# Transposes in row halves of the array over two PSUM banks, and the x1/x2 map once for two half-bands

## The chip, the cores and the metric

The kernel runs on one core of a Trainium2 chip. The metric is device time in microseconds (us), the median of the runs; lower is better. Engines are named as in the profile: PE (TensorE: PE its matmuls, PEld its weight loads), DVE (VectorE), ACT (ScalarE), POOL (GpSimd), SP (the queue that issues most transfers). Everything is float32.

## The reference, cut to what matters

Eight images of 256 channels, 64 x 64 pixels, go through two layers. `_gn` is a group norm without weights.

```python
def layer0(x):                        # on gn(x)
    x1, x2, x3 = w1 x + b1, w2 x + b2, w3 x + b3      # 1x1 maps to 32, 32 and 256 channels
    h = concat(x1, unfold3(reflect_pad(x2)))          # 32 + 288 channels
    h = relu(bn2(cw1 @ relu(bn1(h))))                 # 32 channels
    w = cw2 @ h + cb2                                 # 32 groups x 9 tap weights
    return sum over 9 taps of unfold3(zero_pad(x3)) * w     # 8 channels share a weight
def layer1(x):                        # on gn(x)
    q, k, v = 1x1 maps of x;  4 heads of 64
    att = softmax(q . (unfold7(reflect_pad(k)) + position)) # 49 neighbours of each pixel
    out_att = att . unfold7(reflect_pad(v))
    wts = softmax over 9 taps of (Wfc x)
    oc  = dwconv3(relu(dwconv3(x)))
    return rate1 * out_att + rate2 * sum(wts) * oc    # as the kernel factors it
x = x + layer0(gn(x));  x = x + layer1(gn(x))
```

## The kernel before

An image is cut into 8 bands of 8 rows (512 pixels), so there are 64 bands, counted by `g`. Each turn of the outer loop (L971) does layer 1 for band `g` and, beside it, layer 0 for band `g + 12` (`AHEAD`); the first 12 turns (`g < 0`) have layer 0 alone, the last 12 have no layer 0 left. A turn has 8 **slots**, `s = 4*ct + m`: `ct` is the half of the channels (two heads), `m` a pair of 8 x 8 pixel tiles. The order of all instructions on all engines is written out by hand (`tc.manual_schedule()`): `beside` and `steer` say what is put in the middle (`mid`) or at the end (`end`) of each slot, and `after(n, f)` puts `f` off by `n` calls of `advance()`. Each engine runs its own instructions in that order and never passes one that waits.

A slot of layer 1 puts this on PE, in order:

- `weighted_values` (L735): probabilities times values of an earlier tile pair, in 128 x 64 tiles of the array, two column halves in turn;
- `scores` (L691): queries times keys, in 64 x 64 tiles of the array;
- `transposed` (L723): the probabilities of the slot before, four transposes of 128 x 112 into one PSUM bank (`ptp`), evicted by one ACT copy to `pt` (L725);
- `branch_weights` (L813): four matmul instructions of 512 columns (one product of float32 is two instructions), `pf`, evicted by `exp` on ACT (L818);
- what stands in `mid`; `branch_weights` again; what stands in `end`.

`mid` and `end` hold, over the 8 slots of a band: queries `pq` and keys `pk` (for kb), values `pv` (evicted by several ACT copies to `vc`, L560 to L575), `value_tile` (four transposes of windows of the values, `pvt`, L595, evicted by one ACT copy to `vt`, L597), and of layer 0 the maps `p12` and `p3`, the hidden layer `ph` (L417) and the tap weights `pw` (L435). In an ordinary band `value_tile` stands in the middle of slots 0 and 1 and at the end of slots 6 and 7; `small_maps` (`p12`) stands in the middle of slot 0 behind `value_tile`, `value_maps` (`p3`) at the end of slot 0 and in the middle of slot 1, there behind `value_tile` too.

`small_maps` makes x2 three times and x1 once: `w12` has the columns [w2, w2, w2, w1], so one product of 128 output rows gives three copies of x2, which three ACT instructions write into the tile `x2` with the shifts left, none and right (L332), x1 by a fourth (L335), and two small ones write the reflected edge columns (L337, L338).

All PSUM tiles of PE's products but the scores share one pool, `tag="gen"`, of **five** buffers, each a bank of 2 KB per partition. A tile's first writer waits until the tile that had its bank before has been read.

The softmax of a slot goes PE scores -> DVE masked minimum (L700) -> ACT exp (L708) -> DVE reciprocal (L715) -> ACT scale (L717) -> PE transpose in the next slot. Once per `ct`, `dynamic_sum` (L820 to L849) runs over POOL and DVE, with two reciprocals of 256 columns.

Of the kernel before, what the change touches and what calls it, by code (L numbers as in the profile page):

```python
# [10 lines left out]
F32 = mybir.dt.float32  # L11
BF16 = mybir.dt.bfloat16
AF = mybir.ActivationFunctionType
# [5 lines left out]
P = 128  # L19
C = 256  # L20
NCT = C // P
H = W = 64
HW = H * W
R = 8
BAND = R * W
# [5 lines left out]
REL = 32  # L31
# [14 lines left out]
HD = C // HEADS  # L46
# [40 lines left out]
def conv_layers_kernel(ctx: ExitStack, tc: tile.TileContext, ins: dict, out: bass.AP):  # L87
# [19 lines left out]
    def load(name, shape, src=None, now=True):  # L107
        t = const.tile(shape, F32, name=f"c_{name}")
        late.append(lambda: nc.scalar.dma_start(out=t, in_=ins[name] if src is None else src))
        if now:  # L110
            late.pop()()
        return t
# [2 lines left out]
    par = load("par", [P, NPAR])  # L115
    chan = load("chan", [P, NCT, NCHAN], ins["chan"].rearrange("(t p) n -> p t n", p=P))
    rowp = load("rowp", [P, NROW], ins["rowp"].partition_broadcast(P))
    w12 = load("w12", [P, NCT, P], ins["w12"].rearrange("(t p) n -> p t n", p=P))
    w3 = load("w3", [P, NCT, C], ins["w3"].rearrange("(t p) n -> p t n", p=P))
    c1 = load("c1", [P, 3, REL])  # L120
    gq = load("gq", [P, P])
# [166 lines left out]
    def scaled_weights(b):  # L288

        im = images[b]  # L290

        def scale(sc, bi):
            im.w12s = w0.tile([P, NCT, P], F32, tag="w12s", name=f"w12s_{b}", bufs=1)
            im.w3s = w0.tile([P, NCT, C], F32, tag="w3s", name=f"w3s_{b}", bufs=1)
            for kt in range(NCT):
                nc.vector.tensor_scalar(im.w12s[:, kt], w12[:, kt], sc[:, kt : kt + 1], None, ALU.mult)
                nc.vector.tensor_scalar(im.w3s[:, kt], w3[:, kt], sc[:, kt : kt + 1], None, ALU.mult)
            after(5, lambda: through(bi))

        def through(bi):  # L300
            pb = ps.tile([P, 1 + NCT], F32, tag="gen", name=f"pb_{b}", bufs=5)
            for m, w in enumerate((w12, w3[:, :, :P], w3[:, :, P:])):
                for kt in range(NCT):
                    nc.tensor.matmul(
                        pb[:, m : m + 1], w[:, kt], bi[:, kt : kt + 1], start=(kt == 0), stop=(kt == NCT - 1)
                    )
            after(2, lambda: biases(pb))

        def biases(pb):
            im.bias = w0.tile([P, 1 + NCT], F32, tag="bias", name=f"bias_{b}")  # L310
            nc.vector.tensor_add(im.bias[:, 0:1], pb[:, 0:1], par[:, PB21 : PB21 + 1])
            for ct in range(NCT):
                nc.vector.tensor_add(
                    im.bias[:, 1 + ct : 2 + ct], pb[:, 1 + ct : 2 + ct], chan[:, ct, CB3 : CB3 + 1]
                )

        gn_affine([im.st0[:, ct] for ct in range(NCT)], gmat, f"a{b}", scale)

    def small_maps(b, i):


        im = images[b]
        p12 = ps.tile([P, BAND], F32, tag="gen", name=f"p12_{b}_{i}", bufs=5)
        for kt in range(NCT):
            nc.tensor.matmul(p12, im.w12s[:, kt, :], im.xc[i][:, kt, :], start=(kt == 0), stop=(kt == NCT - 1))  # L325
        p12 = p12.rearrange("p (r c) -> p r c", r=R)
        t = im.x2[i] = w0.tile([P, HR, W], F32, tag="x2", name=f"x2_{b}_{i}", bufs=2)
        bias = im.bias
        for q, (dst, src) in enumerate(((1, 0), (0, 0), (0, 1))):
            n = W - (q != 1)  # L330
            s = slice(32 * q, 32 * q + 32)
            nc.scalar.activation(  # L332
                t[s, 1 : 1 + R, dst : dst + n], p12[s, :, src : src + n], AF.Identity, bias=bias[s, 0:1]
            )
        nc.scalar.activation(t[96:128, 0:R, :], p12[96:128], AF.Identity, bias=bias[96:128, 0:1])  # L335

        nc.scalar.activation(t[0:32, 1 : 1 + R, 0:1], p12[0:32, :, 1:2], AF.Identity, bias=bias[0:32, 0:1])  # L337
        nc.scalar.activation(  # L338
            t[64:96, 1 : 1 + R, W - 1 : W], p12[64:96, :, W - 2 : W - 1], AF.Identity, bias=bias[64:96, 0:1]
        )  # L340

        if i == 0:
            nc.gpsimd.tensor_copy(t[0:96, 0, :], t[0:96, 2, :])
        else:
            nc.gpsimd.tensor_copy(t[0:96, 0, :], im.x2[i - 1][0:96, R, :])
            nc.gpsimd.tensor_copy(im.x2[i - 1][0:96, R + 1, :], t[0:96, 1, :])
        if i == NB - 1:
            nc.gpsimd.tensor_copy(t[0:96, R + 1, :], t[0:96, R - 1, :])
# [184 lines left out]
    def strided(v, at, *dims):  # L533

        return bass.AP(v.tensor, v.offset + at, [v.ap[0], *dims])

    def values(b, j, ct):
# [49 lines left out]
    def value_tile(b, j, u):  # L589
        im = images[b]  # L590
        n = min(R, WP - j * R) * KW
        pvt = ps.tile([CHUNK, 2, C], F32, tag="gen", name=f"pvt_{b}_{j}_{u}", bufs=5)
        for g in range(2):
            for ct in range(NCT):
                nc.tensor.transpose(pvt[:n, g, ct * P : (ct + 1) * P], im.vc[j, ct][:, 2 * u + g, :n], ident)  # L595
        vt = im.vt[j, u] = w1.tile([CHUNK, 2, C], F32, tag="vt", name=f"vt_{b}_{j}_{u}", bufs=9)
        nc.scalar.copy(vt[:n], pvt[:n])  # L597

    def new_keys(i):

# [71 lines left out]

        return finish

    half = [slice(0, HD), slice(HD, P)]
    turn = [0]

    def score_tile(nm):
# [38 lines left out]
            nc.scalar.activation(prob[:, h, :NKEY], prob[:, h, :NKEY], AF.Copy, scale=tot[:, h : h + 1])  # L717

    def transposed(nm, prob):
        ptp = ps.tile([CHUNK, 2, 2, P], F32, tag="gen", name=f"ptp_{nm}", bufs=5)  # L720
        for h in range(2):
            for ch in range(2):
                nc.tensor.transpose(ptp[:, h, ch], prob[:, h, ch * CHUNK : (ch + 1) * CHUNK], ident)  # L723
        pt = w1.tile([CHUNK, 2, 2, P], F32, tag="pt", name=f"pt_{nm}")
        nc.scalar.copy(pt, ptp)  # L725
        return pt

    def weighted_values(b, i, ct, m, pt, sco):
# [305 lines left out]
def _layout(inputs):  # L1034

    a = {k.replace("L0_conv_", "a_").replace("L1_conv_", "b_"): np.asarray(v) for k, v in inputs.items()}
    f = np.float32
    arr = {"x": a["x"].reshape(a["x"].shape[0], C, HW)}
    arr["w12"] = np.concatenate([a["a_w2"].T] * 3 + [a["a_w1"].T], axis=1)
    arr["w3"] = a["a_w3"].T  # L1040

    def branch(v):

        o = np.zeros((P, 3) + v.shape[1:], f)
        u = v[REL:].reshape((REL, 3, 3) + v.shape[1:])
        o[:96] = np.moveaxis(u, 2, 0).reshape((96, 3) + v.shape[1:])
        o[96:, 0] = v[:REL]
        return o

    arr["c1"] = branch(a["a_cw1"].T)  # L1050

    quarter = np.tile(np.eye(REL, dtype=f) / NQR, (NQR, 1))
    arr["gq"] = np.tile(quarter, (1, NQR))
    arr["gc"] = np.repeat(quarter, SHARE, axis=1).reshape(P, NCT, P)
    par = np.zeros((P, NPAR), f)
    for at, n in ((PG, "g"), (PB, "b"), (PM, "m"), (PV, "v")):
        par[:, at : at + 3] = branch(a[f"a_bn1_{n}"])
    par[:, PB21] = np.concatenate([a["a_b2"]] * 3 + [a["a_b1"]])
    for at, n in ((PG2, "g"), (PB2, "b"), (PM2, "m"), (PV2, "v")):
        par[:, at] = np.tile(a[f"a_bn2_{n}"], NQR)  # L1060
    par[:, PCB2 : PCB2 + KK] = np.tile(a["a_cb2"].reshape(REL, KK), (NQR, 1))
    arr["par"] = par

    c2 = a["a_cw2"].reshape(REL, KK, REL).transpose(2, 1, 0)
    arr["c2"] = np.zeros((P, KK, P), f)
    for q in range(NQR):
        arr["c2"][q * REL : (q + 1) * REL, :, q * REL : (q + 1) * REL] = c2

    chan = np.zeros((C, NCHAN), f)
    chan[:, CB3] = a["a_b3"]  # L1070
    chan[:, CBQ] = a["b_bq"]
    chan[:, CBK] = a["b_bk"]
    chan[:, CBV] = a["b_bv"]
    chan[:, CBP] = np.tile(a["b_bp"], HEADS)
    chan[:, CWP0 : CWP0 + 2] = np.tile(a["b_Wp"], (HEADS, 1))
    chan[:, CW1 : CW1 + KK] = a["b_w1"].reshape(C, KK)
    chan[:, CW2 : CW2 + KK] = a["b_w2"].reshape(C, KK)
    arr["chan"] = chan
    arr["wq"], arr["wk"], arr["wv"] = a["b_Wq"].T, a["b_Wk"].T, a["b_Wv"].T

    arr["wfc"] = a["b_Wfc"].reshape(C, KK, C)[:, [0, 1, 2, 3, 5, 6, 7, 8, 4]].transpose(2, 1, 0)

    loc = np.pad(np.linspace(-1.0, 1.0, W, dtype=f), PAD, mode="reflect")
    arr["rowp"] = np.concatenate(
        [loc, a["b_rate1"].reshape(1), a["b_rate2"].reshape(1)]
    )

    arr["gmat"] = np.kron(np.eye(P // 8, dtype=f), np.full((8, 8), 0.125, f))
    q, k = np.arange(NQ), np.arange(NKEY)
    dr = k[None] // KW - q[:, None] // TQ  # L1090
    dc = k[None] % KW - q[:, None] % TQ
    inside = (dr >= 0) & (dr < KA) & (dc >= 0) & (dc < KA)
    arr["mask"] = np.tile(np.where(inside, 0.0, NEG).astype(f), (2, 1))
    return {n: np.ascontiguousarray(v) for n, v in arr.items()}
# [19 lines left out]
```

## Time and profile before

| | us |
|---|---|
| median of 3 runs (4214.88 to 4219.61) | 4218.69 |
| span of the profiled run | 4215.3 |
| PE matmuls busy | 4079.7 (97%) |
| DVE busy | 3582.1 (85%) |
| ACT busy | 3046.5 (72%) |
| POOL busy | 2900.3 (69%) |
| granted TensorE clock, mean | 0.994 |

The busy time of PE counts from a matmul's start to its modelled end, so it holds pipeline latency and is not the rate of the work: the rate is read from the spacing of starts in the timeline. In the groups a row names the line, engine, operation, tile written and read, shape, count, then busy us and mean ns of one, then the idle time just before it and who ended it.

### The profile page before, as it was taken

The numbers are of one execution on the slowest core, as the hardware profiler recorded it, in microseconds if no ns is written. First come the engines' busy times: TensorE is split into PE (matmuls) and PEld (weight loads), VectorE is DVE, ScalarE is ACT, GpSimd is POOL, SyncE is SP. The second block draws the span as 40 slices with busy tenths as digits, with TensorE's granted clock in tenths as the row PEclk, the third lists the DMA queues.
The fourth block names the chain that finished last, engine by engine and source line by source line (L and its number), as shares of the span: only waits on it lengthen the run. The fifth ranks groups of instructions, "written<-read, shape, count | busy, mean of one in ns | idle before, by whom it ended". The sixth has DMA issues, their size and how long they took to land.

```text
span 4215.3 us, 72044 instructions
## 1 busy us (share of the span) xinstructions
PE 4079.7 (97%) x25004; PEld 2134.8 (51%) x25004; DVE 3582.1 (85%) x7244; ACT 3046.5 (72%) x7598; POOL 2900.3 (69%) x1778
## 2 busy tenths in 40 slices
PE   5889999999999999999999999999999999999998
PEld 2445555555555555555555555555555555555554
DVE  5778988888898898888988888888988888977777
ACT  3367778777777777877778777777778777677776
POOL 3657777677776777767777767767777777744445
PEclk9999999999999999999999999999999999999999
DMA  7753334233243333333333333343333233111100
GB/s 219 187 141 101 79 91 106 70 95 98 68 102 95 82 95 85 88 95 95 80 86 104 78 98 88 76 104 88 78 89 89 63 95 77 34 45 39 38 28 21
DMA packets 381260, 367.91 MB, mean 87 GB/s; under 512 B 55392, under 2 KB 282720, under 8 KB 380640
## 3 DMA queue, kind: packets, MB, share of 16 engines
q1 hardware_dynamic: 377568, 358.68, 33.4%
q8 instruction: 199, 3.26, 0.3%
q10 hardware_dynamic: 3328, 4.62, 0.3%
q14 instruction: 165, 1.35, 0.1%
HBM read 261.48 MB, written 101.71 MB: 86 GB/s over the span
## 4 chain that ended last, share of the span: by engine, by line
PE 74%; DVE 12%; POOL 7%; ACT 3%; issue 2%; SPq 2%; DMA 1%; POOLq 0%; ACTq 0%; DVEq 0%
PE pf L813 34%; PE ptp L723 6%; PE sco L735 5%; PE pk L646 5%; PE sco L691 5%; PE p L357 4%; POOL xg L456 4%; DVE prod L448 4%; PE pq L625 3%; PE pv L551 3%; PE pvt L595 2%; PE p L325 2%; PE pw L435 2%; POOL ex L1010 2%; DVE acc L796 2%
## 5 line engine op out<-in xcount | busy, mean ns | idle before, releaser
L813 PE MATMUL pf<-yp,c_wfc 128*128 128x512 f32 x4096 | 1932.4, 595 | 9.3 <-ACT vc L569 4.3
L456 POOL TENSOR_TENSOR xg<-xg,prod 128x1024 f32<-128x1024 f32 x549 | 1203.4, 2192 | 127.4 <-DVE prod L448 104.4
L813 PEld LDWEIGHTS pf<-yp,c_wfc 128*128 128x128 f32 x4096 | 733.8, 191 | 702.7 <-issue 658.9
L1010 POOL TENSOR_TENSOR ex<-ex,ex 128x1024 f32<-128x1024 f32 x384 | 907.7, 2364 | 61.9 <-ACT ex L818 57.2
L818 ACT ACTIVATE ex<-pf 128x512 f32<-128x512 f32 x1024 | 607.2, 593 | 335.7 <-PE pf L813 167.1
L770 DVE SCALAR_TENSOR_TENSOR acc<-yp,c_chan,acc 128x504 f32<-128x504 f32 (+3 forms) x1104 | 766.6, 694 | 47.7 <-ACT acc L761 27.1
L841 POOL TENSOR_TENSOR ex<-ex,rec 128x512 f32<-128x512 f32 x128 | 163.4, 1277 | 914.7 <-DVE rec L836 881.7
L796 DVE SCALAR_TENSOR_TENSOR acc<-hid,c_chan,acc 128x504 f32<-128x504 f32 (+3 forms) x1024 | 758.2, 740 | 20.2 <-ACT acc L790 2.1
L448 DVE SCALAR_TENSOR_TENSOR prod<-pw,c_par,x3q 128x1040 f32<-128x1040 f32 x576 | 734.4, 1281 | 46.3 <-PE pw L435 26.0
L717 ACT ACTIVATE prob<-prob,tot 128x196 f32<-128x196 f32 x1024 | 411.6, 450 | 467.9 <-DVE tot L715 467.9
L700 DVE CUSTOM_DVE_ANT_0 prob<-sco,c_mask 128x196 f32<-128x196 f32 x1024 | 325.1, 355 | 292.5 <-PE sco L691 292.0
L708 ACT ACTIVATE prob<-prob,nmax 128x196 f32<-128x196 f32 x1024 | 462.2, 456 | 46.9 <-DVE nmax L700 46.4
L735 PEld LDWEIGHTS sco<-pt,vt 112*64 112x64 f32 x8160 | 279.2, 137 | 209.5 <-issue 71.4
L723 PE MATMUL ptp<-ident,prob 128*112 128x128 f32 x2044 | 341.3, 287 | 26.4 <-ACT prob L717 25.9
L735 PE MATMUL sco<-pt,vt 112*64 112x64 f32 x8160 | 349.7, 228 | 0.0
L725 ACT COPY pt<-ptp 112x512 f32<-112x512 f32 x511 | 296.2, 580 | 70.5 <-PE ptp L723 66.5
L723 PEld LDWEIGHTS ptp<-ident,prob 128*112 128x112 f32 x2044 | 204.1, 133 | 194.0 <-ACT prob L717 69.4
L691 PE MATMUL sco<-kb,qb 64*64 64x196 f32 x4096 | 294.5, 357 | 0.2 <-DVE kb L661 0.2
L551 PE MATMUL pv<-yp,c_wv 128*128 128x512 f32 (+2 forms) x576 | 251.4, 561 | 0.0
L646 PE MATMUL pk<-yp,c_wk 128*128 128x512 f32 (+2 forms) x576 | 245.0, 552 | 0.0
L625 PE MATMUL pq<-yp,c_wq 128*128 128x512 f32 x512 | 242.2, 596 | 2.3 <-DVE prod L448 2.3
L357 PE MATMUL p<-xc,w3s 128*128 128x512 f32 x512 | 242.7, 598 | 0.0
(136 smaller groups left out, 5288.6 us busy)
## 6 DMA issues: line engine op xcount, KB each, us to landing
x<-x3n SPq DMA_DIRECT2D x128, 264.0 KB, 2.1
x3q<-x SPq DMA_DIRECT2D x128, 264.0 KB, 7.1
xc<-in_x SPq DMA_DIRECT2D x64, 512.0 KB, 5.0
xg<-in_x SPq DMA_DIRECT2D x256, 128.0 KB, 4.8
x<-xg SPq DMA_DIRECT2D x256, 128.0 KB, 2.4
yp<-x SPq DMA_DIRECT2D x128, 256.0 KB, 3.3
xr<-x SPq DMA_DIRECT2D x64, 512.0 KB, 5.7
out_x<-xr SPq DMA_DIRECT2D x64, 512.0 KB, 3.1
```

What stands on the lines that cost most here:

```text
L448: nc.vector.scalar_tensor_tensor(prod[:, :, :RUN], pw[:, j, :RUN].unsqueeze(1).to_broadcast([P, SHARE, RUN]), par[:, PCB2 + k : PCB2 + k + 1],
L456: nc.gpsimd.tensor_add(im.xg[i], im.xg[i], rows(prod))
L646: nc.tensor.matmul(pk[:, :n], wk[:, kt, ct * P : (ct + 1) * P], im.yp[i][:, kt, a : a + n], start=(kt == 0), stop=(kt == NCT - 1),)
L691: nc.tensor.matmul(sco[half[t], h, :NKEY], qb[half[h], 2 * m + t].rearrange("p r c -> p (r c)"), kb[half[h], :, c0 : c0 + KW], start=True, ...
L708: nc.scalar.activation(prob[:, h, :NKEY], prob[:, h, :NKEY], AF.Exp, bias=nmax[:, h : h + 1], scale=-1.0, accum_out=tot[:, h : h + 1],)
L723: nc.tensor.transpose(ptp[:, h, ch], prob[:, h, ch * CHUNK : (ch + 1) * CHUNK], ident)
L735: nc.tensor.matmul(po[half[h], :, t * TQ : (t + 1) * TQ], im.vt[i + ch, m][:n, t, (2 * ct + h) * HD : (2 * ct + h + 1) * HD], pt[:n, h, ch ...
L770: nc.vector.scalar_tensor_tensor(o, yp[:, ct, ra + dr : rb + dr, ca + dc : cb + dc], chan[:, ct, CW1 + k : CW1 + k + 1], o, ALU.mult, ALU.add,
L796: nc.vector.scalar_tensor_tensor(o, hid[:, ra + dr : rb + dr, ca + dc : cb + dc], chan[:, ct, CW2 + k : CW2 + k + 1], o, ALU.mult, ALU.add,)
L813: nc.tensor.matmul(pf, wfc[:, kt, 2 * m + j, ct * P : (ct + 1) * P], images[b].yp[i][:, kt, PAD : PAD + R], start=(kt == 0), stop=(kt == N ...
L818: nc.scalar.activation(ex[:, j].rearrange("p (r c) -> p r c", r=R), pf, AF.Exp)
L1010: after(4, lambda ex=ex, exb=exb: nc.gpsimd.tensor_add(ex, ex, exb))
```

## The change

Three edits, in the same places of the written order.

- `transposed` and `value_tile`: each transpose of 128 rows becomes two of 64 rows. The array is used in two row halves (64 x 128 tiles), upper and lower, one after the other in the instruction stream, so that the two can run side by side; each half writes its own PSUM bank, with 64 columns per transpose instead of 128. The one eviction of 512 columns becomes two of 256.
- `small_maps`: `w12` has the columns [w2, w1] once, 64 of them. The band is cut into two halves of 256 pixels, which go through two column halves of the array (128 x 64 tiles) into the lower and upper 64 partitions of one bank. ACT writes the three shifts and x1 from each half, eight instructions of half the columns; the two edge columns are now copied by POOL from the tile itself.
- The bias products (`pb`) follow the new layout, 8 times in the kernel.

It is for PE time: a transpose streams half the columns, and the map is not made three times over.

```diff
     def transposed(nm, prob):
-        ptp = ps.tile([CHUNK, 2, 2, P], F32, tag="gen", name=f"ptp_{nm}", bufs=5)
+        ptp = [ps.tile([CHUNK, 4, NQ], F32, tag="gen", name=f"ptp_{nm}_{t}", bufs=5) for t in range(2)]
         for h in range(2):
             for ch in range(2):
-                nc.tensor.transpose(ptp[:, h, ch], prob[:, h, ch * CHUNK : (ch + 1) * CHUNK], ident)
+                for t in range(2):
+                    nc.tensor.transpose(
+                        ptp[t][:, 2 * h + ch], prob[half[t], h, ch * CHUNK : (ch + 1) * CHUNK], ident[half[t], half[t]]
+                    )
         pt = w1.tile([CHUNK, 2, 2, P], F32, tag="pt", name=f"pt_{nm}")
-        nc.scalar.copy(pt, ptp)
+        for t in range(2):
+            nc.scalar.copy(pt.rearrange("p h c q -> p (h c) q")[:, :, t * NQ : (t + 1) * NQ], ptp[t])
         return pt
...
     def value_tile(b, j, u):
-        pvt = ps.tile([CHUNK, 2, C], F32, tag="gen", name=f"pvt_{b}_{j}_{u}", bufs=5)
+        pvt = [
+            ps.tile([CHUNK, 2 * NCT, HD], F32, tag="gen", name=f"pvt_{b}_{j}_{u}_{r}", bufs=5) for r in range(2)
+        ]
         for g in range(2):
             for ct in range(NCT):
-                nc.tensor.transpose(pvt[:n, g, ct * P : (ct + 1) * P], im.vc[j, ct][:, 2 * u + g, :n], ident)
-        nc.scalar.copy(vt[:n], pvt[:n])
+                for r in range(2):
+                    nc.tensor.transpose(
+                        pvt[r][:n, g * NCT + ct], im.vc[j, ct][half[r], 2 * u + g, :n], ident[half[r], half[r]]
+                    )
+        for r in range(2):
+            nc.scalar.copy(vt[:n].rearrange("p g (t r d) -> p (g t) r d", r=2, d=HD)[:, :, r], pvt[r][:n])
...
     def small_maps(b, i):
-        p12 = ps.tile([P, BAND], F32, tag="gen", name=f"p12_{b}_{i}", bufs=5)
+        p12 = ps.tile([P, R // 2, W], F32, tag="gen", name=f"p12_{b}_{i}", bufs=5)
         for kt in range(NCT):
-            nc.tensor.matmul(p12, im.w12s[:, kt, :], im.xc[i][:, kt, :], start=(kt == 0), stop=(kt == NCT - 1))
+            for u in range(2):
+                nc.tensor.matmul(
+                    p12[64 * u : 64 * u + 64], im.w12s[:, kt, :],
+                    im.xc[i][:, kt, u * BAND // 2 : (u + 1) * BAND // 2],
+                    start=(kt == 0), stop=(kt == NCT - 1),
+                )
-        for q, (dst, src) in enumerate(((1, 0), (0, 0), (0, 1))):
...
+        for u in range(2):
+            r, o = u * R // 2, 64 * u
+            for q, (dst, src) in enumerate(((1, 0), (0, 0), (0, 1))):
+                n = W - (q != 1)
+                nc.scalar.activation(
+                    t[32 * q : 32 * q + 32, r + 1 : r + 1 + R // 2, dst : dst + n],
+                    p12[o : o + 32, :, src : src + n], AF.Identity, bias=bias[o : o + 32, 0:1],
+                )
...
+        nc.gpsimd.tensor_copy(t[0:32, 1 : 1 + R, 0:1], t[0:32, 1 : 1 + R, 2:3])
+        nc.gpsimd.tensor_copy(t[64:96, 1 : 1 + R, W - 1 : W], t[64:96, 1 : 1 + R, W - 3 : W - 2])
```

## The prediction

> **What bounds the kernel now.** I read the engine shares and the chain first, then the groups that the edits touch, then the timeline of PE.
>
> ```profile
> PE 4079.7 (97%) x25004; PEld 2134.8 (51%) x25004; DVE 3582.1 (85%) x7244; ACT 3046.5 (72%) x7598; POOL 2900.3 (69%) x1778
> PE 74%; DVE 12%; POOL 7%; ACT 3%; issue 2%; SPq 2%; DMA 1%; POOLq 0%; ACTq 0%; DVEq 0%
> L723 PE MATMUL ptp<-ident,prob 128*112 128x128 f32 x2044 | 341.3, 287 | 26.4 <-ACT prob L717 25.9
> L725 ACT COPY pt<-ptp 112x512 f32<-112x512 f32 x511 | 296.2, 580 | 70.5 <-PE ptp L723 66.5
> ```
>
> PE sets the pace: on the chain for 74% of the span, and hardly waiting (26 us before all transposes). But DVE and POOL hold 19% of the chain, so PE meets them somewhere in each band. PE time therefore counts, and so does each new wait of PE. The timeline of PE (start, us, group) gives the prices:
>
> ```profile
> 2005.60 1.88 PE L813 MATMUL pf<-yp,c_wfc 128*128 128x512 f32 x4
> 2007.41 0.43 PE L417 MATMUL ph<-hid,c_c 96*32 96x128 f32 x8
> 2007.77 1.98 PE L551 MATMUL pv<-yp,c_wv 128*128 128x512 f32 x4
> 2009.59 1.88 PE L813 MATMUL pf<-yp,c_wfc 128*128 128x512 f32 x4
> 2011.40 0.69 PE L735 MATMUL sco<-pt,vt 112*64 112x64 f32 x16
> 2012.01 0.57 PE L691 MATMUL sco<-kb,qb 64*64 64x196 f32 x8
> 2012.52 0.65 PE L723 MATMUL ptp<-ident,prob 128*112 128x128 f32 x4
> 2013.00 1.88 PE L813 MATMUL pf<-yp,c_wfc 128*128 128x512 f32 x4
> 2014.72 1.88 PE L551 MATMUL pv<-yp,c_wv 128*128 128x512 f32 x4
> 2016.44 1.88 PE L813 MATMUL pf<-yp,c_wfc 128*128 128x512 f32 x4
> ```
>
> Starts, not durations, are to be read. Four 512-column instructions without a change of tile shape take 1.72 (2014.72 to 2016.44), 0.429 each. Where the next group has another shape they take 1.81 (2005.60 to 2007.41, 2009.59 to 2011.40): **a change of tile shape costs 0.09**. The group after one pays its first weight load too: `pv` after `ph` takes 1.82 instead of 1.72, 0.10 for a 128-column load. The four transposes take 0.48: 0.05 for the first load of 112 columns, then 4 x 0.109. Sixteen instructions of 64 columns in two column halves (L735) take 0.61: 0.05 load, 8 pairs at 0.058, 0.09 change. Two tile halves do run side by side.
>
> **What the Trainium skill says.** "TensorEngine Tiling (Array Packing)", Key Properties: changing the tiling mode drains the engine, changing only the tile doesn't. The trace agrees: 0.09 at each change, nothing between the halves of L735. "TensorE: Matmul & The Clock Gate", Part 3 (The mechanism): matmuls and loads in different row groups overlap; the scores agree (8 instructions in four tiles, two row halves among them, in 0.51, where one stream of 8 x 196 columns at L735's rate would need 1.4). The Tiling page, Gotcha 1, lets different row tiles write only different banks at one time: hence the second bank. "ScalarE: Activation LUTs", What ACT_TABLE_LOAD costs: a fixed part per instruction, about 280 ns with a pointer bias, before 0.833 ns an element; this trace has 265 ns for 8 elements (L338) and 580 for a copy of 512.
>
> **The change part by part.**
>
> *Transposes of probabilities, 511 groups.* Body 4 x 0.109 = 0.436 becomes 4 pairs x 0.058 + 0.006 = 0.24: -0.20. The entry comes from the scores' 64 x 64 tiles and pays 0.09 + 0.05 already. The exit is new: `pf`, today loaded behind the last transpose, now pays 0.09 + 0.10: +0.20. Sum 0.
>
> *Transposes of values, 288 groups.* Body -0.196 x 288 = -56. In the built order 271 of them follow 128 x 128 work and now pay 0.09 + 0.05 at the entry: +39. Of the exits 128 go into L735, which changes shape today as well; 97 go into 128 x 128 work, +0.197 each: +19; 45 go into `p12`, counted there. Sum +2.
>
> *The map of x1 and x2, 64 times.* Four times 0.429 = 1.72 becomes 8 instructions of 256 columns in pairs, 4 x 0.216 = 0.86; entry 0.09 + 0.05, exit 0.09 + 0.10. Net -0.51. The 12 in the turns without layer 1 aren't on PE's path (PE is busy 190 of the first 269 us): 52 x -0.51 = -26.
>
> PE's own work: about -24 us.
>
> *ACT.* A copy of 128 x 252 takes 353 ns in the trace, one of 512 columns 580. Two halves are about 0.72: +0.14 a group, 799 groups, +112 us. `p12`: today 2 x 672 + 680 + 679 + 2 x 265 = 3.23; eight of 256 columns at 265 + 0.82 x 250 = 470 are 3.76: +34 us in all. ACT goes from 3046 to about 3190, 76%. It is not the bound, but it is later wherever PE waits for it. The two POOL copies of an edge column take at most the 0.23 of the 96 x 64 copy in the trace, 30 us on an engine 69% busy: hidden beside the products.
>
> *Banks.* This is the part that sets the sign. The pool has five, and a transpose group now takes two, so a tile gets a bank that was handed out fewer tiles ago. I took each tile's bank in the built program of the changed kernel and, with the times of before, the end of the last read of its former tenant against the start of its first write. In an ordinary band all but a few keep 0.6 us or more; those that come out negative stand in the same slots of every band:
>
> ```profile
> 2338.13 0.81 ACT L717 ACTIVATE prob<-prob,tot 128x196 f32<-128x196 f32 x2 [5.18 <-DVE tot L715]
> 2338.64 0.78 PE L723 MATMUL ptp<-ident,prob 128*112 128x128 f32 x4 [1.16 <-ACT prob L717]
> 2339.26 1.88 PE L813 MATMUL pf<-yp,c_wfc 128*128 128x512 f32 x4
> 2339.92 0.34 ACT L569 COPY vc<-pv 128x16 f32<-128x16 f32 x3
> 2347.11 0.58 ACT L818 ACTIVATE ex<-pf 128x512 f32<-128x512 f32 x1
> 2347.26 1.98 PE L813 MATMUL pf<-yp,c_wfc 128*128 128x512 f32 x4
> 2347.59 0.58 ACT L597 COPY vt<-pvt 112x512 f32<-112x512 f32 x1
> ```
>
> ACT stands for 5.18 us behind DVE's reciprocal, then works off what has piled up. In slot 6 `pf` (2339.26) gets the bank of `pv`, read until 2340.26: PE starts it at 2340.4. In slot 7 the second transpose tile gets the bank of slot 6's second `pf` (read until 2347.69) and `pf` that of the first half of `pvt` (until about 2347.95). So transposes end near 2348.0, and `pf` streams at 2348.2 after drain and load, where today it streams at 2347.37: **+0.83 a band**, since ACT and DVE here wait for no PE and don't move. Queued behind these waits is all of PE; who waits for PE comes later and moves with it. With bands 0 to 5 of images 0 to 6: 42 x 0.83 = +35. In bands 6 and 7 the gaps are -0.45 and -0.5: +7.
>
> In band 0 ACT waits for DVE in front of the copies of two value tiles:
>
> ```profile
> 2284.47 0.65 PE L723 MATMUL ptp<-ident,prob 128*112 128x128 f32 x4
> 2286.33 0.22 ACT L776 ACTIVATE hid<-acc 128x64 f32<-128x64 f32 x1 [1.65 <-DVE acc L770]
> 2287.22 1.06 ACT L597 COPY vt<-pvt 112x512 f32<-112x512 f32 x2
> ```
>
> The second `ptp` gets the bank of a half of `pvt`, free at about 2287.6: PE stands from 2284.5 on, +3.1; 8 images, +25. Last, `pf` of slot 1 gets the bank of `p12`, whose ACT reading ends about 1 later (0.14 + 0.14 + 0.53 and a little queueing) while PE arrives 0.5 sooner; the gap of 1.24 becomes about -0.25: 52 x 0.25 = +13.
>
> Waits: +80. Sum: 4218.7 - 24 + 80, about **4273 us**.
>
> **The rivals.**
>
> *PE's saving stands, the waits don't come* (faster). For it: PE waits little today, and my gaps hold ACT's times fixed. Against: at the two places ACT is held by DVE, not by PE. 4218.7 - 24 = 4195.
>
> *ACT becomes the pace in the crowded slots.* For it: L725 waits only 66 us for PE today, so ACT is often behind; two fifths of the 146 us added to it might then reach PE, 60. Against: in the stage from 1000 to 3500 it is busy 1876 of 2500. 4273 + 60 = 4335.
>
> *The halves don't run side by side* (the two row halves take turns): 8 x 0.058 = 0.46 a body instead of 0.24, 799 x 0.225 = +180: 4450. Against: the scores use row halves side by side.
>
> *Gain and waits cancel*: a third of the waits (26) would do: about 4220.
>
> **How the numbers follow.** My forecast 0.60, ACT pacing 0.14, no side by side 0.07: slower 0.81. Waits absent 0.14: faster. Cancelling: same 0.05. Unknown costs: a pair at 0.055 to 0.07 moves the sum by -10 to +38 us, a half copy at 0.33 to 0.42 moves ACT by -48 to +96 us, of which waits pass on perhaps half. The range 4190 to 4335 takes in the first rival and the unknown costs and leaves out the 4450 and the upper part of ACT's case.
>
> **What would show it.** Right: starts of L723's successor 0.24 + 0.05 after its own group, plus 0.19 before the next stream; the count of such exits at 511; waits of PE before `ptp` and `pf` put down to ACT (`vt`, `vc`, `ex`) of some 80 us more than today, about 0.8 in slot 7 of each band and 3 in slot 0 of each image's first; `p12` in 0.86. Wrong: pairs at 0.11 (no overlap), no 0.09 at the exit (then faster by up to 100 us), or PE's waits unchanged.

## The result, and the profile after

| | before | after |
|---|---|---|
| median, us | 4219.15 | 4279.4 |
| lowest and highest run | 4214.88 to 4219.94 | 4277.57 to 4281.49 |
| span of the profiled run | 4215.3 | 4276.7 |
| granted TensorE clock, mean | 0.994 | 0.985 |

The ratio is 1.0145, with a 95% interval of 1.0127 to 1.0163: the changed kernel is slower by 60 us. The forecast was 4273. Each column has four runs; for the kernel before that is one run more than ahead of the prediction, so its median is 4219.15 instead of 4218.69.

The lines of the page of the changed kernel that answer to those shown of before (engine shares, chain, groups):

```profile
PE 4080.4 (95%) x28492; PEld 2042.7 (48%) x28492; DVE 3586.4 (84%) x7244; ACT 3127.8 (73%) x8526; POOL 2925.0 (68%) x1906
PE 52%; DVE 24%; POOL 10%; ACT 6%; issue 4%; DMA 2%; SPq 2%; POOLq 0%; DVEq 0%; ACTq 0%
L746 ACT COPY pt<-ptp 112x256 f32<-112x256 f32 x1022 | 326.3, 373 | 58.3 <-PE ptp L741 57.9
L741 PE MATMUL ptp<-ident,prob 64*112 64x64 f32 x4088 | 247.1, 231 | 53.8 <-ACT vt L614 19.3
```

PE's busy time hardly changed (4079.7 to 4080.4) although the map costs less. PE's share of the chain fell from 74% to 52%, so it now waits in places where it did not wait before. The transposes stand 53.8 us before they start (26.4 before). The list of PE's waits (what waits, for whom, us in total, times, longest) of the changed kernel says for whom:

```profile
PE pf L834 <- ACT vc L579: 35.8, 36, 1.0
...
PE ptp L741 <- ACT vt L614: 19.3, 7, 2.8
PE ptp L741 <- ACT prob L733: 14.3, 16, 2.3
PE ptp L741 <- ACT ex L839: 7.1, 33, 0.4
```

The same lines of the kernel before:

```profile
PE ptp L723 <- ACT prob L717: 25.9, 51, 2.7
...
PE pf L813 <- ACT vc L569: 4.3, 6, 0.7
```

Only `prob` is data that the transposes read. `vc`, `vt` and `ex` are ACT's copies *out of* the banks that PE wants to write: these are waits for a bank, 36 of them of 1.0 us behind the values' copies (6 of at most 0.7 us before), 7 of 2.8 us behind the value tiles. The prediction had named both banks. One of the 36, in the timeline of the changed kernel, first PE and then ACT:

```profile
2374.32 0.67 PE L741 MATMUL ptp<-ident,prob 64*112 64x64 f32 x8 [1.12 <-ACT prob L733]
2375.99 3.52 PE L834 MATMUL pf<-yp,c_wfc 128*128 128x512 f32 x4 [0.99 <-ACT vc L579]
2379.30 2.08 PE L642 MATMUL pq<-yp,c_wq 128*128 128x512 f32 x4
```

```profile
2366.27 0.68 ACT L746 COPY pt<-ptp 112x256 f32<-112x256 f32 x2
...
2373.81 0.81 ACT L733 ACTIVATE prob<-prob,tot 128x196 f32<-128x196 f32 x2 [5.14 <-DVE tot L731]
2374.53 0.70 ACT L570 COPY vc<-pv 128x672 f32<-128x672 f32 x1
2375.25 0.31 ACT L575 COPY vc<-pv 128x176 f32<-128x176 f32 x1
2375.60 0.34 ACT L579 COPY vc<-pv 128x16 f32<-128x16 f32 x3
```

The first ACT line, two half evictions, is used further down. The products of this `pv` had started at 2367.81 and PE went on to its next group at 2369.53, but ACT copied them only from 2374.53 on: the scale ahead of them waited 5.14 us for DVE's reciprocal. `pf` starts at 2375.99, when the last `vc` copy (2375.60 + 0.34) has emptied the bank of `pv`. There is a second thing to see, which no step of the prediction has: from the start of this `pf` to the next group pass 3.31 us, where the same four instructions took 1.82 elsewhere. PE runs at half its clock here. The table by stretches, with the granted clock in the column before the DMA share, shows it: first the changed kernel,

```profile
core 0: us, PE busy (x) PEld busy (x) DVE busy (x) ACT busy (x) POOL busy (x), PEclk, DMA share, GB/s
...
2318.00:2321.40 3.40, 3.18 (x10) 1.63 (x11) 3.25 (x7) 2.42 (x10) 2.40 (x2) 0.54 0.80 215
2376.00:2379.40 3.40, 3.40 (x5) 1.39 (x6) 3.40 (x8) 3.17 (x9) 2.30 (x2) 0.54 0.02 5
```

then the kernel before in the second stretch:

```profile
2376.00:2379.40 3.40, 3.40 (x34) 1.80 (x33) 3.30 (x9) 3.40 (x7) 3.32 (x3) 1.00 0.99 320
```

**Where the time went.** Two sums over the whole trace carry the rest of this document. *Waits*: for each of the 511 transpose groups, the time from the start of the scores before it to the start of `pf` behind it, less the median of all groups of that kernel. (This takes in a wait before the first transpose, between two of them, and before `pf`.) *Half clock*: the time at a granted clock of 0.5, without the first 300 and the last 20 us; each costs PE half of itself at most. All rows but `before` and `after` are kernels of the experiments below; an interval is mostly 3.4 us long, some are 6.8.

```
                         median   waits   of which in:             half clock
                         us       us      slots 6, 7  band 0,      us (intervals)
                                                      slots 0, 1
before                   4219      55.5      54.2        0.0         3.4  (1)
map_only                 4194.5    55.5      53.8        0.3         6.8  (1)
ptp_only                 4252.1    85.1      80.4        0.7        30.7  (8)
pvt_only                 4280.7    92.1      71.3       18.1        23.9  (6)
two_banks                4294.7   104.0      82.6       18.9        47.8 (13)
two_copies               4216.5    55.1      53.7        0.0         3.4  (1)
after                    4279.4   128.5      93.3       24.0        61.4 (17)
values_first             4307.5   130.3      97.5       22.2       109.2 (31)
late_scale               4230.3    85.6      51.6       23.8        47.8  (8)
tiles_first              4257.7   112.5      94.5        7.4        41.0  (9)
late_scale_tiles_first   4202.1    68.5      51.3        6.5         3.4  (1)
before_late_tiles        4204.0    46.2      43.6        0.0         0.0  (0)
map_late_tiles           4179.8    45.8      43.2        0.5         3.4  (1)
```

From before to after: waits +73, half clock (61.4 - 3.4) / 2 = +29 at most, PE's own work about -39 (52 maps at -0.507, 511 transpose groups at -0.0175, and in 52 bands the value tiles, with slot 1 longer by 0.125 and slots 0, 6 and 7 shorter by 0.07 each: -4). That makes +63 at most where the span grew by 61; some 2 us of the half-clock cost lie inside the groups whose waits are summed, and are counted twice.

### The profile page after: what moved, and what is told of

It reads as the page before. It is cut to its first block, busy times and chain, and to the rows that moved or that the text cites. A ratio compares the mean times of both kernels' runs of the same rounds, so it can differ in the third digit from the quotient of the medians.

```text
span 4276.7 us, 79947 instructions
## 1 busy us (share of the span) xinstructions
PE 4080.4 (95%) x28492; PEld 2042.7 (48%) x28492; DVE 3586.4 (84%) x7244; ACT 3127.8 (73%) x8526; POOL 2925.0 (68%) x1906
## 4 chain that ended last, share of the span: by engine, by line
PE 52%; DVE 24%; POOL 10%; ACT 6%; issue 4%; DMA 2%; SPq 2%; POOLq 0%; DVEq 0%; ACTq 0%
PE pf L834 26%; POOL xg L464 5%; DVE prod L456 5%; PE pk L663 5%; DVE acc L817 4%; DVE acc L791 4%; PE p L365 4%; PE sco L756 4%; PE pq L642 3%; PE sco L707 3%; POOL ex L1031 3%; DVE ex L852 3%; PE ptp L741 2%; DVE rec L853 2%; POOL ex L845 1%
## 5 line engine op out<-in xcount | busy, mean ns | idle before, releaser
L834 PE MATMUL pf<-yp,c_wfc 128*128 128x512 f32 x4096 | 2013.7, 615 | 42.8 <-ACT vc L579 35.8
L746 ACT COPY pt<-ptp 112x256 f32<-112x256 f32 x1022 | 326.3, 373 | 58.3 <-PE ptp L741 57.9
L741 PE MATMUL ptp<-ident,prob 64*112 64x64 f32 x4088 | 247.1, 231 | 53.8 <-ACT vt L614 19.3
L741 PEld LDWEIGHTS ptp<-ident,prob 64*112 64x112 f32 x4088 | 164.0, 131 | 221.0 <-issue 54.1
```

What stands on the lines that cost most here:

```text
L741: nc.tensor.transpose(ptp[t][:, 2 * h + ch], prob[half[t], h, ch * CHUNK : (ch + 1) * CHUNK], ident[half[t], half[t]])
L834: nc.tensor.matmul(pf, wfc[:, kt, 2 * m + j, ct * P : (ct + 1) * P], images[b].yp[i][:, kt, PAD : PAD + R], start=(kt == 0), stop=(kt == N ...
```

## The experiments

Theories for the loss: **B** (banks), PE waits for banks because a transpose group takes two of the five; **A** (ACT), the larger number of ACT instructions is the price; **R** (row halves), the changes of tile shape cost more than the shorter transposes save. Each ratio is to runs of the kernel before made beside that run (medians 4217.81 to 4219.2).

**The map alone** (`map_only`): before with the edits to `small_maps`, `w12` and `pb` and no others.

> The map of x1 and x2 alone in its new form, the transposes as before. My theory: PE saves 0.51 us in each of the 52 bands that have layer 1 beside it, no tile gets a bank sooner than before but for small shifts, so 4219 - 26, about 4193 (4188 to 4200). Rival, that the longer ACT reading of the map's bank takes the gain back in slot 1: 4210 or more.

4194.52 us (4192.56 to 4199.17), ratio 0.9946 (0.9933 to 0.9958). As expected: slot 0 of an ordinary band is 0.507 us shorter, and the waits stay at 55.5. This part of the change is a gain in full.

**The transposes of probabilities alone** (`ptp_only`): before with the edit of `transposed` and no others.

> The transposes of probabilities alone in row halves over two banks. My theory: PE -9 us (511 x 0.017, from the trace after), waits of about 0.45 us at slot 7 in 42 bands (+20) and about 1.1 us in the first band of each image (+9), so about 4240 (4228 to 4255). Rival, that the new changes of tile shape are what costs and not the banks: the waits of PE for ACT stay as before and the spacing behind each transpose group is over 0.3 us longer than the body saves.

4252.07 us (4251.37 to 4254.49), ratio 1.0081 (1.0067 to 1.0094). Within the expected range, but not by the expected sum. Slots without a wait are 0.017 us *shorter*, so a group's gain in the body and its exit nearly cancel, and the waits are +29.6 as expected, though nearly all in slots 6 and 7 (+26) and hardly any in band 0 (+0.7, where 9 were expected). The rest is seven more half-clock intervals, (30.7 - 3.4) / 2 = 14 us, which were not expected.

**The transposes of values alone** (`pvt_only`): before with the edit of `value_tile` and no others.

> The transposes of values alone in row halves over two banks. My theory: PE's own work -3 us, waits of 2.8 us in slot 0 of each image's first band (+23), 0.44 us at slot 7 in 42 bands (+18), so about 4257 (4240 to 4268). Rival, that all of the loss hangs on the probabilities, which are twice as many: 4220.

4280.65 us (4279.66 to 4281.57), ratio 1.0147 (1.0133 to 1.0161): 24 us over what was expected, and outside the range. A line of its list of waits:

```profile
PE ptp L731 <- ACT qb L638: 42.8, 41, 1.2
```

In slot 7 the transposes now wait for the bank that ACT's copy of the queries (`qb`) empties. The waits grew by 36.6, half of that in band 0, half in slots 6 and 7; 41 were expected. So the miss lies elsewhere. Alone, PE's own work is not level but about +10 by the prediction's own prices: 271 entries at 0.14 are +38, and of exits into full-shape work there are now 142 (97 and the 45 into the unchanged `p12`) at 0.197, +28, against -56. Slots 0 and 1 show it, each 0.125 us longer. With the half clock's 10 that is 57 of the 63; the other 6 stay open.

**Two banks without row halves** (`two_banks`): the kernel before, with four full-height transposes spread over two banks and two evictions, for the probabilities as shown and for `value_tile` likewise.

```diff
-        ptp = ps.tile([CHUNK, 2, 2, P], F32, tag="gen", name=f"ptp_{nm}", bufs=5)
+        ptp = [ps.tile([CHUNK, 2, P], F32, tag="gen", name=f"ptp_{nm}_{t}", bufs=5) for t in range(2)]
...
-        nc.scalar.copy(pt, ptp)
+        for h in range(2):
+            nc.scalar.copy(pt[:, h], ptp[h])
```

> Kernel before, with each group of four full-height transposes spread over two banks and evicted by two ACT copies: the banks and the copies of the change without its row halves and without any new change of tile shape. My theory (the banks set the sign): all waits of the changed kernel come, 42 x 0.9 + 8 x 3 + 7, so about 4289 (4270 to 4300). Rival (the row halves and their shape changes cost the time): 4219 to 4225.

4294.74 us (4292.9 to 4298.19), ratio 1.0182 (1.0166 to 1.0197). The two largest bank waits of the changed kernel are there, in the same counts, in its list of waits:

```profile
PE pf L815 <- ACT vc L569: 28.0, 36, 0.8
...
PE ptp L724 <- ACT vt L598: 15.9, 7, 2.3
```

PE's instructions are those of the kernel before (only the order of the four transposes differs), the tile shape changes nowhere else than it did before, and yet it loses 77 us. R is out as the cause of the loss. (That the new exits eat the gain of the shorter transposes is so: `ptp_only` has -0.017 a group left of 0.20.) The 4289 that was expected was met partly by luck: the waits grew by 48.5 and not by 69, and the half clock adds (47.8 - 3.4) / 2 = 22.

**Two evictions, one bank** (`two_copies`): before, with each eviction of a transpose group (`ptp` and `pvt`) cut in two, the bank as it was.

```diff
-        nc.scalar.copy(pt, ptp)
+        for h in range(2):
+            nc.scalar.copy(pt[:, h], ptp[:, h])
```

> Kernel before, with every eviction of a transpose group cut into two ACT copies from the same one bank: the added ACT work of the change without a second bank. My theory: ACT works 80 to 110 us more in all, and PE hardly sees it: 4216 to 4225. Rival (ACT's added work is what PE waits for): half of it comes through, 4260 or more.

4216.45 us (4213.48 to 4219.15), ratio 0.9996 (0.9987 to 1.0005): nothing. The copies of the groups take 48 us more on ACT than before, as they do in the changed kernel (47); its whole busy time rose by 43, less than the expected 80 to 110. `map_only` holds the rest of ACT's added work, without a loss. A is out. The second bank is what `two_banks` has and `two_copies` has not.

**Values' copies ahead of the scale** (`values_first`): the changed kernel; in slot 5, ACT gets the copies of `pv` before it waits for DVE's reciprocal.

```diff
+                rest = [f() for f in mid] if s == 5 else None
                 if g >= 0:
                     probabilities(prob, tot)
-                rest = [f() for f in mid]
+                if rest is None:
+                    rest = [f() for f in mid]
```

> The changed kernel, with the copies of pv in slot 5 ahead of the scaling of the probabilities on ACT, so that pv's bank is free before DVE's reciprocal. My theory: the wait of pf in slot 6 (about 1 us a band, 36 us in all put down to vc) goes away, and comes back in slot 7, where ptp and pf wait for the banks of pq, of slot 6's second pf and of pvt, all read by ACT behind the next reciprocal: 4270 to 4281. Rival (the waits of slots 6 and 7 add up, so one of them can be had by itself): 42 x 1.1 less, about 4233.

4307.51 us (4299 to 4310.33), ratio 1.0207 (1.019 to 1.0224): missed, slower than the changed kernel by 28. The wait went from slot 6 to slot 7 of the same band, -1.1 and +1.2 us on average over the 42 bands, and the sum of waits is nearly the same (130.3 against 128.5), so that half of the theory held. But the 28 us are no waits. What differs is the clock: 31 half-clock intervals instead of 17, (109.2 - 61.4) / 2 = 24 us. Behind its transposes, slot 7 is longer by 1.3 to 1.7 us, up to half an interval, in 23 of the 42 bands. This run showed what the prediction had left out.

**ACT's scale behind the copies** (`late_scale`): the changed kernel; in slots 5 and 6 the reciprocal stays where it was and ACT's scaling of the probabilities goes behind the copies of `mid` and the second `exp`.

```diff
-                    probabilities(prob, tot)
+                    probabilities(prob, tot, "reciprocal" if s in (5, 6) else None)
...
                     branch_weights(b, i, ct, m, 1, ex)
+                    if s in (5, 6):
+                        probabilities(prob, tot, "scale")
```

> The changed kernel, with ACT's scaling of the probabilities put behind the copies of the slot's middle and behind the exp of its second pf, in slots 5 and 6 (DVE's reciprocal stays where it is). Then no bank read in these slots stands behind the reciprocal. My theory: both waits go, 42 x about 1, less some 10 us where the reciprocal is early and the scaling now waits for pf (bands 6, 7 and the last image): about 4240 (4230 to 4252). Rival (the waits are DVE's lateness itself and not the banks): no gain, 4275 or more.

4230.33 us (4224.47 to 4235.08), ratio 1.003 (1.0017 to 1.0043), at the lower edge of the range. ACT no longer stands for DVE with the copies queued behind it; the waits of slots 6 and 7 fall from 93.3 to 51.6, below the kernel before (54.2).

**Value tiles first at an image's end** (`tiles_first`): the changed kernel; the instructions in `end` of the last slot of an image go ahead of the depthwise stage's first ones, so that ACT copies `vt` before the `hid` that waits for DVE.

```diff
+                early = s == 7 and (g + 1) % NB == 0
+                if early:
+                    for f in end:
+                        f()
...
-                for f in end:
+                for f in () if early else end:
```

> The changed kernel, with the value tiles at the end of an image ahead of depthwise_begin, so that their ACT copies don't stand behind DVE. My theory: the 3 us in slot 0 of each image's first band go (8 x 2.5 = 20 us), and since the first depthwise pass begins about 1.3 us later on DVE some of it comes back: 4268 (4255 to 4275). Rival (that wait isn't the banks of pvt): 4278 or more.

4257.66 us (4255.02 to 4266.06), ratio 1.0097 (1.0082 to 1.0112): within the range, with twice the gain that was expected. The waits of band 0 shrink from 24.0 to 7.4 us in all (0.06 instead of 3.3 in slot 0 of an image, and 0.95 now in slot 1), and the half-clock time falls from 61.4 to 41.0 us (9 intervals of 17), worth up to 10 us of the 22 gained.

**Both reorderings, in three kernels**: the changed kernel (`late_scale_tiles_first`), the kernel before (`before_late_tiles`), and before with the map (`map_late_tiles`). The diffs are the two above.

> The changed kernel with both reorderings: ScalarE's scaling of the probabilities behind the copies and the second exponential in slots 5 and 6, and the value tiles of the next image ahead of the depthwise stage's first instructions at an image's end. If the two waits are independent, as their places say (slots 5 and 6 of each band; slot 7 of an image's last band), the gains add: 4230 - 22 = 4208, 4200 to 4220, so the row halves in two banks are then a gain of about 10 over the kernel before. If the gain of the one comes from the same clock intervals as that of the other, or the wait at the image's end moves to another engine, 4218 to 4230.

> The kernel before with the same two reorderings and nothing else. Its own list of waits has 25.9 us of transposes that wait for probabilities and no wait of the image's end of note. If the reorderings repair only what the second bank takes, 4212 to 4222 (none). If they take away waits that the kernel before has as well, 4195 to 4210, and then the row halves are judged against this time and not against the kernel before.

> The kernel before with the x1/x2 map made once for a band (4194.5 when alone) and the two reorderings, no row halves. If the parts add, 4194.5 less whatever the reorderings give the kernel before: 4180 to 4195. Under the theory that the second bank, not the row halves, is what the reorderings repair, this is the quickest of all kernels here, ahead of the changed kernel with the same reorderings by 15 to 30; if the row halves are worth their price once the waits are gone, it is behind or level with it.

| | us | runs | ratio to before, interval |
|---|---|---|---|
| `late_scale_tiles_first` | 4202.07 | 4201.28 to 4203.42 | 0.9962 (0.995 to 0.9975) |
| `before_late_tiles` | 4203.97 | 4200.36 to 4204.61 | 0.9965 (0.9952 to 0.9977) |
| `map_late_tiles` | 4179.75 | 4178.46 to 4181.85 | 0.9908 (0.9893 to 0.9923) |

The changed kernel gains 77 us by the two reorderings, more than the sum of the two alone (49 + 22). The waits add up (-43 and -16 alone, -60 together), but nearly all half-clock time goes as well: 61.4 us, 47.8 or 41.0 with one of them, 3.4 with both. Slot 6 of a band then looks so in its timeline, with nothing left of the two waits of a microsecond but 0.2:

```profile
2389.09 0.67 PE L742 MATMUL ptp<-ident,prob 64*112 64x64 f32 x8
2389.69 1.98 PE L835 MATMUL pf<-yp,c_wfc 128*128 128x512 f32 x4
2391.51 1.88 PE L642 MATMUL pq<-yp,c_wq 128*128 128x512 f32 x4
```

The kernel before gains only 15 by the same edits: so they mend most of all what the second bank broke, and a little that was there before. And the row halves with their second bank are still not worth it: `map_late_tiles`, which has all but them, is 22.3 us faster than `late_scale_tiles_first`, as was expected (15 to 30), and its waits are 22.7 us less. It is the fastest kernel of this study, 39 us faster than before.

## Why the prediction was right, step by step

- *Body and exit of the transposes of probabilities, sum 0*: right. In the timeline of the changed kernel the group takes 0.37, exit included (forecast 0.05 + 0.24 + 0.09), and the `pf` behind it pays 0.10 for its load and 0.09 for the next change (1.91 instead of 1.72):

```profile
2002.38 0.44 PE L741 MATMUL ptp<-ident,prob 64*112 64x64 f32 x8
2002.75 1.98 PE L834 MATMUL pf<-yp,c_wfc 128*128 128x512 f32 x4
2004.66 0.44 PE L610 MATMUL pvt<-ident,vc 64*112 64x64 f32 x8
2005.03 1.08 PE L328 MATMUL p<-xc,w12s 128*64 128x256 f32 x8
2006.05 1.98 PE L834 MATMUL pf<-yp,c_wfc 128*128 128x512 f32 x4
```

  The slots without a wait came out at -0.0175 us instead of 0, 511 times: -9 us, from pairs slightly quicker than the 0.058 taken from the weighted values.
- *Transposes of values, +2*: right to within what the slots show, in all about -4. Slot 1, with an exit into full-shape work, is longer by 0.12 (forecast 0.134), slots 6 and 7, before the weighted values, shorter by 0.07 each (forecast 0.056).
- *The map, -26*: right. It takes 1.02 with its exit (2005.03 to 2006.05), and `map_only` has -0.507 a band and -23 in all.
- *ACT, +146*: too high. It rose by 81 (3046.5 to 3127.8). A half copy lasts 373 ns, as forecast, but the next one starts before the first has ended: two take 0.68 from the first start to the last end in the group at 2366.27, not 0.75, and 0.64 on average (326.3 us over 511 groups). The 799 groups took 47 us more instead of 112; the instructions for `p12` took 31 more, near the forecast 34. The Trainium skill has this ("ScalarE: Activation LUTs", What ACT_TABLE_LOAD costs: back-to-back instructions overlap by about 93 ns), and the trace has about as much (2 x 0.373 - 0.64 = 0.11 us); the prediction cites this passage for the price of an instruction and left the overlap out. The slip cost the forecast nothing, since it let none of ACT's added time reach PE but through the banks, and `two_copies` shows that ACT's part alone is free.
- *Banks, slots 6 and 7, +42*: right in sum. The waits there rose by 39.1, and the table of before's bank ends, laid against the built order of the changed kernel, gave the tenants. In the 42 bands it is +37.7 (forecast 35), in the other bands +1.4 (forecast 7). The sign that was named, some 0.8 more in slot 7 of each band, isn't what the trace has: slot 6 waits 1.07 more on average and slot 7 0.17 *less*. The two belong together: what PE has waited for in slot 6 it needn't wait for again in slot 7, where it stood for `prob` before (10.9 us in 35 of the 42 slots, none after). The sum of a band, 0.90, is the forecast 0.83.
- *Banks, band 0, +25*: right, +24.0: 3.2 us in slot 0 of each image but the first (2.9 in the last), and 1.6 in slot 1 of the first, where 3.1 was forecast for each of the 8.
- *`pf` of slot 1 behind the bank of `p12`, +13*: right in place, half in size. From the start of the transposes to `pf` pass 0.48 us there in an ordinary band where slots 0 and 2 to 5 have 0.366: 0.11 a band instead of 0.25. `pf`'s weight load waits there for the last read of `p12` (L343), 45 times.
- *Sum of waits, +80*: +73 was measured.
- *The clock*: missing in the prediction. 16 more intervals at half clock are worth up to 29 us, half of the whole loss. The 15 us that PE gained beyond the forecast (39 instead of 24) and the waits that came out 7 smaller nearly make up for it. So the sign and the waits were understood, but that the sum is off by only 6 is in part luck.
- *Arithmetic*: a few sums of the prediction don't come out of their terms. 4218.7 - 24 + 80 is 4274.7 and not 4273, and 4273 + 60 is 4333 and not 4335; the map's own prices give -0.52 and not -0.51; 271 entries at 0.14 are 38 and not 39. None of it bears on the outcome.

Of the rivals, "the waits don't come" and "gain and waits cancel" fall by the table, "no halves side by side" by the 0.37 of a group. That two row halves need two banks, on which the layout rests, was taken as given: no run here lets both write one bank. "ACT becomes the pace" would have come to 4335; `two_copies` disproves it. The parts alone add up to -23 + 34 + 63 = +74, more than the +60 of all. One cause is in the numbers: 45 groups of value transposes leave into `p12`, which in the full change has its own change of shape to pay anyway (45 x 0.197 = 9). The waits are no cause: they are 66 in the two parts and 73 together, more in the whole. So the rest of the difference stays open, with the 6 us of `pvt_only`.

## What to carry to other kernels

An edit that saves on the bounding engine but takes a second buffer of a shared pool is judged by the pool: lay the last read of each former tenant against the first write of the new one, and look for the places where the reading engine stands for a third one; a wait of one microsecond there in each band costs more than all transposes save. Then try to move the copies that empty the buffers ahead of the instruction that waits, and look where the wait goes: `late_scale` got 49 us back so, `values_first` lost 28. Look at the clock along with the waits: here two waits of a microsecond close together were often followed by an interval at half clock, which costs up to 1.7 us more.

## What the runs showed of the hardware that was not expected

The intervals at half clock are 3.413 us long (or twice that) and start on a grid of that length through the whole trace: in the changed kernel those at 1287.44 and 2318.26 lie 302 grid steps apart. The first 300 and the last 20 us are again left out. I cut each trace into windows on this grid and took the time in each in which no matmul was in flight. A window at full clock, and the one after it:

```
                         idle in windows that        largest idle in windows
                         a half-clock one follows    followed by full clock
before                   2.11                        1.36
after                    1.31 to 2.79 (17)           1.06
two_banks                1.18 to 2.27 (13)           1.51
values_first             1.24 to 2.78 (31)           1.42
late_scale_tiles_first   2.14                        1.14
before_late_tiles        none                        1.78
map_late_tiles           2.32                        1.33
```

So in these traces a window at full clock with less than about 1.2 us without a matmul was followed by full clock, one with more than about 1.5 by half clock, and in between both occur. Two windows stand outside: the 1.78 in the table, and one of 1.05 in `tiles_first` that a half-clock one did follow. In a window already at half clock less was enough: in all thirteen traces 0.58 us or more was followed by a second window at half clock (15 of 15), 0.55 or less by full clock (97 of 97). Of `late_scale`'s 8 intervals 6 are such doubles.

The Trainium skill ("TensorE: Matmul & The Clock Gate", Part 1) has the free-running window of about 3.4 us and the two rates, and the trace agrees with both; but its table ties the drop to an idle window of about 3.4 us, and here in many cases less than half a window without a matmul went before it (1.2 to 1.7 us). The measurement decides.

In the changed kernel slot 6 has 1.12 and 0.99 us of waits with 0.6 us of small transposes between: 2.1 in a window, if both fall into the same one. This would also explain `values_first`: its intervals come 64.85 us apart over and over (1294.0, 1358.8, 1423.7, 1488.5), which is 19 windows. From slot 7 to slot 7 the first two bands of an image take 62.9 to 63.0 us there without such an interval, and 64.6 to 64.7 with one; so each interval, by the 1.7 us that it costs, brings the wait of the next band to nearly the same place on the grid. A wait's price then hangs on the length of the band, which no view of one band shows.

That the clock follows the waits was not tried by itself (a wait added with nothing else changed); it is read from thirteen traces.
